# Neighbour lists of a sparse attention layer: 32 strided chunks of 104 columns in place of 52 contiguous chunks of 64

## The chip, the cores and the metric

The kernel runs on one core of a Trainium2 chip. Its time is the device time of one execution, in microseconds (us); the number to judge by is the median of several executions. The profile is one execution recorded by the hardware profiler. Engines are named as there: PE is TensorE, DVE is VectorE, ACT is ScalarE, POOL is GpSimd, SP is SyncE.

## The reference

Four graph attention layers run over n = 3327 nodes with 256 features. The adjacency matrix is given as int32, symmetric, with every node its own neighbour, and sparse: about 33 neighbours per row. Only layer 0 is touched here. It computes

```
g_src = x @ W_src.T + b_src
g_tgt = x @ W_tgt.T + b_tgt
g     = leaky_relu(g_src[:, None, :] + g_tgt[None, :, :], 0.2)
score = einsum('ijc,c->ij', g, a_w)
score = where(adj != 0, score, -inf)
x     = layernorm(x + softmax(score, axis=1) @ g_tgt)
```

The nonlinearity stands between the sum and the product with a_w, so the score of a pair (i, j) can't be split into a part of i and a part of j: each pair costs work over 256 features. Layers 1 to 3 are attention layers whose scores can be split; they are computed densely.

## The kernel before

Layer 0 (`sparse0`) works on the pairs that exist. The nodes are cut into 26 tiles of 128 rows (the last has 127), and the tiles into three sets of 5, 9 and 12 (`SETS`).

`targets` computes g_tgt for each tile and writes it, with one more number per row, to `table_d` in DRAM, 260 numbers per row. The last tile's missing row becomes row n of the table, with a penalty of -1e6: a place in a list that holds no neighbour points there.

`neighbours(s)` makes the lists of one set, one tile after the other. Each half of the adjacency rows (1664 columns) is loaded, and L402 multiplies "is a neighbour" with a descending number, n minus the column, in uint16, so that each neighbour is a distinct positive number and the rest is 0. The same instruction adds the row's numbers up into `sums`. Then the diagonal is taken out (L411, L415). The DVE's MAX8 gives the 8 largest numbers of a row. L421 takes them from each of 52 chunks of 64 adjacent columns. The 3 largest of each chunk (`FIRST`) go to `few` (L426), and the 8 largest of all the fourth to eighth ones too (L430): 52 x 3 + 8 = 164 candidates. L433 and L435 take the 56 largest (`KMAX`) out of `few` in 7 rounds of 8. L440 and L443 subtract what was found from the row's sum; a remainder would set `lost`. At the very end, a branch repeats everything densely (`dense0`) if any row lost a neighbour. L445 turns numbers back into table rows.

Within a set, rows are then sorted by their number of neighbours: PE spreads a key of each row (L466), L475 counts the larger ones, and the lists are written to DRAM in that order (`write_list`, L488) and read back (`read_lists`, L496). Sorting lets each tile of the sorted order gather only as many places as its longest list needs (`LEVELS`), 923 gathers in all.

A gather (L527) is an indirect transfer issued by POOL: for one place of the list it fetches a table row for each of 128 rows. Eight places make a part; 11 buffers hold parts. `score` on DVE takes maxima (L546), multiplies with a_w and sums (L552), and adds a column of the table to the scores (L607). `combine` makes the softmax: DVE finds the largest score (L618), ACT scales the gathered rows (L633) and PE adds them up (L636).

The order on PE, DVE, ACT and POOL is the program's order inside `sparse0`; nothing is moved by a scheduler there. The lists of set 0 are made first, each step of `neighbours(0)` behind one tile of `targets`. Then a loop goes over the parts: in each turn it runs as many steps of the next sets' `neighbours` as are needed to have the lists in time, issues the gather four parts ahead, and scores the current part. `neighbours` gives way 6 times per tile: in the middle and at the end of each half's chunks, after the rounds of `found`, and after the sort key. A set's lists are written by POOL between gathers.

Of the kernel before, what the change touches and what calls it, by code (L numbers as in the profile page):

```python
# [8 lines left out]
F32 = mybir.dt.float32  # L9
# [5 lines left out]
ALU = mybir.AluOpType  # L15
# [4 lines left out]
P = 128  # L20
# [5 lines left out]


KMAX = 56
CHUNK = 64
FIRST = 3  # L30


SETS = (5, 9, 12)
# [13 lines left out]
def gat_stack(  # L47
# [51 lines left out]

    h = [nodes.tile([P, dim], F32, name=f"h{it}") for it in range(nt)]  # L100
    at_d = dram.tile([nt * P, n], BF16, name="at_d")
    table_d = dram.tile([nt * P, ROW], F32, name="table_d")

    def copy_rows(engine, dst, src):

# [141 lines left out]

    def sparse0(lost):  # L250
        GROUP, TURNS, LEAD = 8, 11, 4
        starts = [sum(SETS[:s]) for s in range(len(SETS))]
        with ExitStack() as s0:
# [33 lines left out]
            for lo, hi in halves:  # L287
                hi = -(-hi // P) * P
                rev_i = io0.tile([P, nt * P // 2], I32, tag="adj_i", name="rev_i")
                nc.gpsimd.iota(  # L290
                    rev_i[:, : hi - lo], pattern=[[-1, hi - lo]], base=n - lo,
                    channel_multiplier=0,
                )
                nc.vector.tensor_copy(rev[:, lo:hi], rev_i[:, : hi - lo])
# [37 lines left out]
            def targets(it):  # L332

                xt, pn = columns_of(it)
                row = io0.tile([P, ROW], F32, tag="row", name="row", bufs=3)
                nc.vector.memset(row[:, dim:], 0.0)
                if pn < P:
                    nc.vector.memset(row[:, :dim], 0.0)
                    nc.vector.memset(row[:, dim : dim + 1], -FAR)
                pt = ps0.tile([P, BANK], F32, tag="acc", name="pt")  # L340
                project(pt, xt, pn, w_tgt)
                yield
                nc.vector.tensor_add(row[:pn, :dim], pt[:pn, :dim], bt_row[:pn])
                nc.scalar.copy(row[:pn, dim : dim + 1], pt[:pn, dim : dim + 1])
                nc.scalar.dma_start(table_d[it * P : (it + 1) * P, :], row)
                nc.scalar.dma_start(own_rows(it)[:, 2 * dim :], row)
                yield

# [23 lines left out]
            ]  # L372

            len_c = nt * P // CHUNK

            def neighbours(s):

# [7 lines left out]
                for t in range(size):  # L385
                    it = starts[s] + t
                    pn = rows_of(it)
                    before, of_rows = of_rows, sources(it)
                    cand = io0.tile([P, len_c, 8], F32, tag="cand", name="cand")
                    sums = io0.tile([P, 4], F32, tag="sums", name="sums")  # L390
                    if pn < P:
                        nc.vector.memset(sums, 0.0)
                    for b, (lo, hi) in enumerate(halves):
                        w, padded = hi - lo, -(-(hi - lo) // P) * P
                        adj_i = io0.tile([P, nt * P // 2], I32, tag="adj_i", name="adj_i")
                        copy_rows(nc.sync, adj_i[:pn, :w], adj[it * P : it * P + pn, lo:hi])
                        v = io0.tile([P, wider], U16, tag="num", name="num")
                        if pn < P:
                            nc.vector.memset(v, 0.0)
                        elif w < padded:  # L400
                            nc.vector.memset(v[:, w:padded], 0.0)
                        nc.vector.scalar_tensor_tensor(  # L402
                            v[:pn, :w], adj_i[:pn, :w], 0.0, rev[:pn, lo:hi],
                            op0=ALU.not_equal, op1=ALU.mult, accum_out=sums[:pn, b : b + 1],
                        )
                        if lo <= it * P < hi:

                            at0 = it * P - lo
                            own_v = v[:, at0 : at0 + P]
                            junk = io0.tile([P, P], F32, tag="junk", name="junk")  # L410
                            nc.vector.scalar_tensor_tensor(  # L411
                                junk, own_v, -1.0, ident, op0=ALU.mult, op1=ALU.mult,
                                accum_out=sums[:, 2:3],
                            )
                            nc.vector.tensor_mul(own_v, own_v, off_diag)  # L415
                        chunks = padded // CHUNK
                        for c in range(chunks):
                            if c == chunks // 2:
                                next(of_rows if b else before, None)
                                yield  # L420
                            nc.vector.max(  # L421
                                cand[:, lo // CHUNK + c, :], v[:, c * CHUNK : (c + 1) * CHUNK]
                            )
                        yield
                    few = io0.tile([P, FIRST * len_c + 8], F32, tag="few", name="few")
                    nc.vector.tensor_copy(  # L426
                        few[:, : FIRST * len_c].rearrange("p (c f) -> p c f", f=FIRST),
                        cand[:, :, :FIRST],
                    )
                    nc.vector.max(few[:, FIRST * len_c :], cand[:, :, FIRST:])  # L430
                    found = io0.tile([P, KMAX], F32, tag="found", name="found")
                    for r in range(0, KMAX, 8):
                        nc.vector.max(found[:, r : r + 8], few)  # L433
                        if r + 8 < KMAX:
                            nc.vector.match_replace(  # L435
                                out=few, in_to_replace=found[:, r : r + 8], in_values=few,
                                imm_value=0.0,
                            )
                    yield
                    nc.vector.tensor_reduce(  # L440
                        sums[:, 3:4], found, axis=AX.X, op=ALU.add, negate=True
                    )
                    nc.vector.tensor_reduce(lost[:, it : it + 1], sums, axis=AX.X, op=ALU.add)  # L443
                    payload = io0.tile([P, KMAX + 2], U32, tag=f"pay{t}", name="payload", bufs=1)
                    nc.vector.tensor_scalar(  # L445
                        payload[:, :KMAX], found, -1.0, float(n), op0=ALU.mult, op1=ALU.add
                    )
                    nc.vector.tensor_copy(payload[:, KMAX : KMAX + 1], own_i[:, it : it + 1])
                    nc.vector.tensor_scalar_mul(
                        payload[:, KMAX + 1 :], sums[:, 2:3], -1.0  # L450
                    )
                    payloads.append(payload)

                    junk = io0.tile([P, P], F32, tag="junk", name="junk")
                    count = io0.tile([P, 1], F32, tag="count", name="count")
                    nc.vector.tensor_scalar(
                        junk[:, :KMAX], found, 0.0, 0.0, op0=ALU.is_gt, op1=ALU.add,
                        accum_out=count,
                    )
                    nc.vector.scalar_tensor_tensor(  # L460
                        keys[:, t : t + 1], count, 4096.0, own_f[:, it : it + 1],
                        op0=ALU.mult, op1=ALU.subtract,
                    )
                    key_diag = io0.tile([P, P], F32, tag="key_diag", name="key_diag")
                    nc.vector.tensor_scalar_mul(key_diag, ident, keys[:, t : t + 1])  # L465
                    nc.tensor.matmul(  # L466
                        key_rows[:, t * P : (t + 1) * P], ones, key_diag, start=True, stop=True
                    )
                    yield
# [93 lines left out]
            def score(q):  # L563
# [6 lines left out]
                if k0 == 0:  # L570
                    sc = entry["sc"] = io0.tile([P, KMAX + 1], F32, tag="sc", name="sc", bufs=3)
                    if kt < KMAX:
                        at = nt + starts[s] + t
                        nc.vector.tensor_scalar(
                            lost[:, at : at + 1], entry["lst"][:, kt : kt + 1], float(n), None,
                            op0=ALU.is_lt,
                        )

                    y_own = io0.tile([P, 1, dim], F32, tag="y_own", name="y_own", bufs=1)
# [129 lines left out]
            def finish(s):  # L709
                mv, rstd = moments.pop(s)  # L710
                for k in range(SETS[s]):
                    it = starts[s] + k
                    pn = rows_of(it)
                    nc.vector.tensor_scalar(
                        h[it][:pn], h[it][:pn], mv[:pn, k, 0:1], rstd[:pn, k : k + 1],
                        op0=ALU.subtract, op1=ALU.mult,
                    )


            first = neighbours(0)  # L720
# [782 lines left out]
```

The softmax here doesn't subtract the row's maximum and nothing guards it: scores larger than these inputs give would overflow.

## Time and profile before

| what | value |
|---|---|
| median of 3 executions | 3261.68 us (3260.0 to 3262.12) |
| span of the profiled execution | 3261.5 us |
| PE busy | 2224.4 us, 68% of the span |
| DVE busy | 2318.1 us, 71% |
| POOL busy | 1029.6 us, 32% |
| first and last gather (L527) | 166.9 us and 1515.0 us |
| MAX8 over chunks (L421) | 1352, mean 209 ns |
| MAX8 and MATCH_REPLACE8 over `few` (L433, L435) | 182 and 156, mean 332 and 313 ns |

The shares over the span mix stages: up to about 1515 us the kernel is in layer 0, after it in the dense layers, where PE is nearly always busy. A stage has to be read by itself. The durations of DVE's instructions overlap, one starting before the one before it has ended, so a group's count times its mean is more than its busy time. A row of the view of waits reads: engine, what it was about to do, the work it waited for, the time in all, how often, the longest.

### The profile page before, as it was taken

The numbers are of one execution on the slowest core, as the hardware profiler recorded it, in microseconds if no ns is written. First come the engines' busy times: TensorE is split into PE (matmuls) and PEld (weight loads), VectorE is DVE, ScalarE is ACT, GpSimd is POOL, SyncE is SP. The second block draws the span as 40 slices with busy tenths as digits, with TensorE's granted clock in tenths as the row PEclk, the third lists the DMA queues.
The fourth block names the chain that finished last, engine by engine and source line by source line (L and its number), as shares of the span: only waits on it lengthen the run. The fifth ranks groups of instructions, "written<-read, shape, count | busy, mean of one in ns | idle before, by whom it ended". The sixth has DMA issues, their size and how long they took to land.

```text
span 3261.5 us, 44647 instructions
## 1 busy us (share of the span) xinstructions
PE 2224.4 (68%) x15644; PEld 1218.1 (37%) x15644; DVE 2318.1 (71%) x6589; ACT 741.5 (23%) x2002; POOL 1029.6 (32%) x1034
## 2 busy tenths in 40 slices
PE   3203332343441444343899999999999999999997
PEld 2101111121220221111478888774334444334342
DVE  6789999999975655554235642117888788899998
ACT  0003231342341343333334431110111110110110
POOL 0077657777767777774000000000000000000000
PEclk7556666666765776676699999999999999999998
DMA  7466536555435444443466753332212212212111
GB/s 216 137 141 180 169 100 150 173 157 155 112 86 109 124 111 113 113 113 91 125 199 199 201 161 93 100 99 72 63 44 68 61 46 65 63 49 57 56 47 48
DMA packets 176842, 364.21 MB, mean 112 GB/s; under 512 B 33746, under 2 KB 118964, under 8 KB 176610
## 3 DMA queue, kind: packets, MB, share of 16 engines
q1 hardware_dynamic: 96682, 183.56, 19.8%
q0 software_dynamic: 49632, 141.57, 16.9%
q10 hardware_dynamic: 30296, 36.15, 3.2%
q8 instruction: 126, 2.06, 0.3%
q14 instruction: 106, 0.87, 0.1%
HBM read 320.99 MB, written 43.58 MB: 112 GB/s over the span
## 4 chain that ended last, share of the span: by engine, by line
PE 46%; DVE 4%; DMA 2%; ACT 1%; issue 1%; DVEq 0%; SPq 0%; POOL 0%; ACTq 0%; POOLq 0%
PE acc L1198 17%; PE acc L1159 15%; PE acc L1206 8%; PE misc L1011 3%; DVE e L1075 3%; PE misc L1048 1%; DMA at_i<-in_adj_t_dram 1%; PE misc L1104 1%; DMA at<-at_d 1%; PE misc L1280 0%; PE misc L1241 0%; PE acc L636 0%; DVE stats L1355 0%; DVE h L1353 0%; ACT feat L1023 0%
## 5 line engine op out<-in xcount | busy, mean ns | idle before, releaser
L527 POOL DMA_INDIRECT g<-table_d,lst x923 | 912.6, 989 | 295.6 <-issue 268.8
L1075 DVE SCALAR_TENSOR_TENSOR e<-rate,feat,at 128x896 f32<-128x896 f32 (+4 forms) x832 | 843.1, 1078 | 67.7 <-PE acc L1206 58.4
L636 PE MATMUL acc<-g,ident 128*128 128x512 f32 (+1 forms) x934 | 454.7, 644 | 545.2 <-ACT g L633 512.7
L1198 PE MATMUL acc<-e,feat 128*32 128x384 f32 (+2 forms) x6656 | 722.8, 514 | 5.2 <-DVE e L1075 2.4
L225 POOL TENSOR_TENSOR rstds<-rstds,minus_half 128x7 f32<-128x7 f32 (+1 forms) x12 | 19.6, 1633 | 1671.7 <-DVE rstds L224 1671.7
L636 PEld LDWEIGHTS acc<-g,ident 128*128 128x128 f32 x934 | 193.3, 211 | 783.7 <-ACT g L633 561.6
L546 DVE TENSOR_TENSOR y<-g,both 128x1024 f32<-128x1024 f32 (+2 forms) x240 | 276.0, 1173 | 238.4 <-DMA g<-table_d,lst 223.5
L1206 PE MATMUL acc<-e,feat 128*32 128x384 f32 (+3 forms) x3328 | 397.5, 512 | 0.0
L1198 PEld LDWEIGHTS acc<-e,feat 128*32 128x32 f32 x6656 | 245.1, 109 | 381.8 <-issue 262.5
L633 ACT ACTIVATE g<-g,w 128x256 f32<-128x256 f32 x923 | 370.6, 494 | 0.0
L552 DVE SCALAR_TENSOR_TENSOR y<-y,both 128x256 f32<-128x256 f32 x923 | 324.5, 415 | 0.0
L1159 PE MATMUL acc<-feat,e 128*128 128x257 f32 (+2 forms) x1352 | 307.4, 381 | 0.6 <-DVE h L1173 0.6
L1159 PEld LDWEIGHTS acc<-feat,e 128*128 128x128 f32 (+2 forms) x1352 | 253.2, 190 | 39.7 <-issue 4.1
L1159 PE MATMUL acc<-feat,at 128*128 128x257 bf16 (+2 forms) x2028 | 240.9, 276 | 7.5 <-DMA at<-at_d 7.3
L466 PE MATMUL key_rows<-key_diag,ones 128*128 128x128 f32 x52 | 17.8, 440 | 314.5 <-DVE key_diag L465 259.5
L1159 PEld LDWEIGHTS <-at 128*128 128x128 bf16 (+2 forms) x2028 | 200.2, 100 | 43.9 <-DMA at<-at_d 8.0
L1075 DVE SCALAR_TENSOR_TENSOR e<-rate,feat,at_i 128x896 f32<-128x896 f32 (+2 forms) x104 | 112.2, 1081 | 143.1 <-DMA at_i<-in_adj_t_dram 109.8
L1206 PEld LDWEIGHTS acc<-e,feat 128*32 128x32 f32 (+1 forms) x3328 | 136.1, 110 | 164.2 <-issue 150.4
L421 DVE MAX8 cand<-num 128x8 f32<-128x64 uint16 x1352 | 178.9, 209 | 1.0
L542 ACT COPY both<-own_of 128x256 f32<-128x256 f32 x26 | 9.7, 374 | 602.1 <-DMA own_of<-own_d,lst 469.2
L466 PEld LDWEIGHTS key_rows<-key_diag,ones 128*128 128x128 f32 x52 | 12.1, 278 | 327.8 <-DVE key_diag L465 216.0
L1092 ACT CAST at<-at_i 128x896 bf16<-128x896 int32 (+2 forms) x104 | 92.0, 885 | 108.5 <-DMA at_i<-in_adj_t_dram 104.2
(158 smaller groups left out, 1707.5 us busy)
## 6 DMA issues: line engine op xcount, KB each, us to landing
at<-at_d SPq DMA_DIRECT2D x150, 224.0 KB
at_i<-in_adj_t_dram SPq DMA_DIRECT2D x50, 448.0 KB
adj_i<-in_adj_dram SPq DMA_DIRECT2D x25, 832.0 KB
adj_i<-in_adj_dram SPq DMA_DIRECT2D x25, 831.5 KB
g<-table_d,lst POOLq DMA_INDIRECT x923, 2.8
at<-at_d SPq DMA_DIRECT2D x75, 192.0 KB
at<-at_d SPq DMA_DIRECT2D x75, 191.8 KB
at_d<-at ACTq DMA_DIRECT2D x50, 224.0 KB
```

The source lines that it names most:

```text
L421: nc.vector.max(cand[:, lo // CHUNK + c, :], v[:, c * CHUNK : (c + 1) * CHUNK])
L527: nc.gpsimd.indirect_dma_start(out=g[:, k - k0, :], out_offset=None, in_=table_d[:, :], in_offset=bass.IndirectOffsetOnAxis(ap=entry["lst" ...
L546: nc.vector.tensor_tensor(y, rows, minus_src[:, None, :].to_broadcast([P, m, dim]), op=ALU.max)
L552: nc.vector.scalar_tensor_tensor(y, y, 1.0, a, op0=ALU.mult, op1=ALU.mult, accum_out=sc)
L633: nc.scalar.activation(rows, rows, AF.Copy, scale=w[:, k : k + 1])
L636: nc.tensor.matmul(dst, ident, rows, start=start, stop=stop)
L1011: nc.tensor.matmul(pacc[:pn, : dim + nh], ht[:, k, :pn], self.weight[:, k, :], start=(k == 0), stop=(k == kc - 1),)
L1075: nc.vector.scalar_tensor_tensor(e[:pn, : c1 - c0], self.rate[b][:pn, h_of, : c1 - c0], q, at[:pn, : c1 - c0], op0=ALU.max, op1=ALU.mult,)
L1092: nc.scalar.copy(at[:pn, :w], at_i[:pn, :w])
L1159: nc.tensor.matmul(accs[s][:pn, : dim + 1], a[:pj, s * P : s * P + pn], f[:pj, : dim + 1], start=(j == 0 and part == 0), stop=(j == nt - 1 ...
L1198: nc.tensor.matmul(accs[x][p][q : q + 32, : hi - lo], f[:pj, at0 : at0 + 32], es[at0 // hd][:pj, lo:hi], start=(j == 0), stop=(j == nt - 1),)
L1206: nc.tensor.matmul(accs[x][pairs][h_of * 32 : (h_of + 1) * 32, : hi - lo], f[:pj, dim + h_of : dim + h_of + 1].to_broadcast([pj, 32]), es[ ...
```

## The change

A chunk becomes 104 columns, so there are 32 and not 52. A chunk's columns are no longer adjacent: in a half with 16 chunks, chunk c holds columns c, c + 16, c + 32 and so on. Adjacent chunks of this length would have more rows with many neighbours in one chunk. `few` then has 32 x 3 + 8 = 104 candidates, and one more: the row's sum less the sum of the candidates. If just one neighbour is not among the candidates, this difference is that neighbour's number. A bound keeps it in range where several are missing, which the check on `lost` still finds.

For the numbers to be told from sums more easily they are now 4096 plus the column, ascending, so a list runs from high columns to low ones. The absent neighbour becomes row 0 of the table, all real rows move down by one, and the row with the penalty is written once at the start. The list arithmetic follows.

```diff
-CHUNK = 64
+CHUNK = 104
 FIRST = 3
+BASE = 4096
...
-    table_d = dram.tile([nt * P, ROW], F32, name="table_d")
+    assert n <= BASE
+    table_d = dram.tile([n + 1, ROW], F32, name="table_d")
...
-                    rev_i[:, : hi - lo], pattern=[[-1, hi - lo]], base=n - lo,
+                    rev_i[:, : hi - lo], pattern=[[1, hi - lo]], base=BASE + lo,
...
-                    nc.vector.memset(row[:, dim : dim + 1], -FAR)
...
-                nc.scalar.dma_start(table_d[it * P : (it + 1) * P, :], row)
+                nc.scalar.dma_start(table_d[1 + it * P : 1 + it * P + pn, :], row[:pn])
...
                         chunks = padded // CHUNK
+                        spread_v = v[:, :padded].rearrange("p (i c) -> p c i", c=chunks)
...
                             nc.vector.max(
-                                cand[:, lo // CHUNK + c, :], v[:, c * CHUNK : (c + 1) * CHUNK]
+                                cand[:, lo // CHUNK + c, :], spread_v[:, c, :]
                             )
                         yield
-                    few = io0.tile([P, FIRST * len_c + 8], F32, tag="few", name="few")
+                    few = io0.tile([P, FIRST * len_c + 9], F32, tag="few", name="few")
...
-                    nc.vector.max(few[:, FIRST * len_c :], cand[:, :, FIRST:])
+                    nc.vector.max(few[:, FIRST * len_c : FIRST * len_c + 8], cand[:, :, FIRST:])
+
+                    nc.vector.tensor_reduce(
+                        sums[:, 3:4], few[:, : FIRST * len_c + 8], axis=AX.X, op=ALU.add, negate=True
+                    )
+                    lack = few[:, FIRST * len_c + 8 :]
+                    nc.vector.tensor_reduce(lack, sums, axis=AX.X, op=ALU.add)
+                    nc.vector.tensor_scalar_min(lack, lack, float(BASE + n - 1))
...
-                        payload[:, :KMAX], found, -1.0, float(n), op0=ALU.mult, op1=ALU.add
+                        payload[:, :KMAX], found, 1.0 - BASE, 0.0, op0=ALU.add, op1=ALU.max
...
-                            lost[:, at : at + 1], entry["lst"][:, kt : kt + 1], float(n), None,
-                            op0=ALU.is_lt,
+                            lost[:, at : at + 1], entry["lst"][:, kt : kt + 1], 0.0, None,
+                            op0=ALU.is_gt,
...
+            none = io0.tile([1, ROW], F32, tag="pen", name="none")
+            nc.vector.memset(none, 0.0)
+            nc.vector.memset(none[:, dim : dim + 1], -FAR)
+            nc.scalar.dma_start(table_d[0:1, :], none)
```

More of the change, by code (lines that the diff above doesn't have):

```diff
@@ L374, in sparse0 @@
             len_c = nt * P // CHUNK
+            assert all((-(-hi // P) * P - lo) % CHUNK == 0 for lo, hi in halves)
             def neighbours(s):
```

## The prediction

> **What bounds the kernel now.** I read the page's 40 slices first (VectorE, the DVE, fills its slices up to about 900 us and TensorE only from 1600 us on), then cut the span into stages and asked for each engine's busy time in each:
>
> ```profile
> 26.00:142.00 116.00, 45.91 (x122) 31.25 (x122) 101.56 (x519) 3.98 (x25) 0.19 (x1) 0.63 0.58 172
> 142.00:190.00 48.00, 0.00 (x1) 0.04 (x1) 22.87 (x113) 0.75 (x2) 26.15 (x26) 0.50 0.35 98
> 190.00:905.00 715.00, 253.94 (x568) 122.54 (x568) 694.34 (x3044) 186.81 (x478) 507.65 (x492) 0.65 0.54 148
> 905.00:1515.00 610.00, 244.22 (x512) 109.88 (x512) 348.65 (x1309) 212.39 (x544) 462.24 (x485) 0.69 0.43 112
> 1515.00:3261.00 1746.00, 1674.41 (x14426) 949.90 (x14426) 1145.96 (x1592) 336.16 (x951) 25.80 (x17) 0.97 0.32 91
> ```
>
> The columns are stage, length, then PE, PEld, DVE, ACT and POOL busy. From 26 to 142 us DVE works 101.56 of 116 us, on the lists of the first 5 tiles. From 190 to 905 us it works 694.34 of 715 us (97%): the lists of the other 21 tiles, mixed with scores. From 905 us on DVE has air, and GpSimd's queue (POOL) issues one gather each 1.25 us to the end of layer 0. Everything after 1515 us is layers 1 to 3, which the change doesn't touch. So the question is what POOL waits for before 905 us. The view of its waits says:
>
> ```profile
> POOL lists_d L488 <- DVE ranks_i L479: 133.7, 1, 133.7
> POOL lists_d L488 <- DVE lost L574: 24.8, 1, 24.8
> POOL lists_d L488 <- DVE inv L658: 11.5, 1, 11.5
> ```
>
> Each of the three sets ends with one wait of POOL for DVE's ranks, before it may write the lists (L488). In the timeline the second ends at 431.98 us, just after ranks_i at 431.53, though the row names a neighbour instruction; the third ends at 905.71. A longer DVE lengthens all three one for one. A shorter one can take back no more than the wait that is there: 11.5 us in the last set.
>
> **What one DVE instruction costs.** Duration isn't what counts, as instructions overlap; the distance between starts is. From the timeline and the groups by form:
>
> ```profile
> 28.41 1.74 DVE L421 MAX8 cand<-num 128x8 f32<-128x64 uint16 x13
> 38.49 0.43 DVE L430 MAX8 few<-cand 128x8 f32<-128x260 f32 x1
> 38.95 0.33 DVE L433 MAX8 found<-few 128x8 f32<-128x164 f32 x1
> 44.29 0.20 DVE L440 TENSOR_REDUCE sums<-found 128x1 f32<-128x56 f32 x1
> 44.53 0.16 DVE L443 TENSOR_REDUCE lost<-sums 128x1 f32<-128x4 f32 x1
> ```
> ```profile
> L421 DVE MAX8 cand<-num 128x8 f32<-128x64 uint16 x1352 | 178.9, 209 | 1.0
> ...
> L607 DVE TENSOR_TENSOR sc<-sc,g 128x2 f32<-128x2 f32 x3 | 0.5, 161 | 0.1
> L607 DVE TENSOR_TENSOR sc<-sc,g 128x4 f32<-128x4 f32 x2 | 0.3, 166 | 0.1
> L607 DVE TENSOR_TENSOR sc<-sc,g 128x7 f32<-128x7 f32 x1 | 0.2, 171 | 0.0
> L618 DVE TENSOR_REDUCE top<-sc 128x1 f32<-128x57 f32 x3 | 0.6, 211 | 0.1
> L618 DVE TENSOR_REDUCE top<-sc 128x1 f32<-128x27 f32 x1 | 0.2, 181 | 0.0
> ```
>
> Thirteen MAX8 of 64 elements take 1.74 us with the last one's 0.209, so one follows the other after (1.74 - 0.21)/12 = 127 ns. An adjacent element costs 1.04 ns on this engine: L546 takes 411 ns for 256 and 1214 for 1024, and L618 gives (211 - 181)/30 = 1.0. So 127 ns is 67 for 64 elements and 60 fixed.
>
> L607 is the row that decides this case. It adds column dim of the gathered rows, elements that lie 1040 bytes apart. From 2 to 7 of them it grows by 10 ns, 2.0 each; a line through its rows of 2 to 7 (161, 163, 166, 169, 168, 171) gives 1.94. That is about two cycles of 1.04 for each element that lies alone. The new chunks read v with a step of 16 uint16, 32 bytes, so here too no two elements are neighbours.
>
> [...]
>
> **The change, part by part, for one tile of 128 rows.**
> - Chunk search (L421): before 52 x 127 = 6.60 us. After, 32 of 104 elements. At two cycles: 60 + 104 x 2.08 = 276 ns, 32 x 276 = 8.84 us, +2.24. At one cycle: 60 + 108 = 168 ns, 5.38 us, -1.22. I take two cycles, for a measured row of this engine stands behind it.
> - Search in few: 164 candidates become 105, 59 x 1.04 = 61 ns off each of 7 MAX8 (L433) and 6 MATCH_REPLACE8 (L435), both contiguous at one element per cycle: -0.80. L430 reads 160, not 260: -0.10. The copy L426 moves 96, not 156, about -0.03.
> - Three new instructions, each waiting for the one before, and the first MAX8 of few queued behind them. The sum over 104: L440 to L443 is 0.24 us for 56, plus 48 x 1.04 = 0.05: 0.29. The sum over 4: 0.157 as L443 and the same 0.035 of hand-over: 0.19. The minimum, like L449 (0.15) with a hand-over: 0.19. Together +0.67.
> - All but the chunks: 0.67 - 0.93 = -0.26 us. With two cycles +1.98 us per tile, with one -1.48.
> - The list arithmetic (L445, L574) keeps its instructions and shapes, so costs nothing. The absent row is written once at the start: two memsets and one small transfer, while DVE waits 15.5 us for the first adjacency. The last table transfer now has 127 rows; the last issue is at 122.6 us and the first gather at 166.9, so even a transfer several times slower stays hidden behind the ranks and the lists.
> - The gathers stay 923. Lists now run downward, which changes the rows' order and not their number.
> - The fallback branch runs only if a list lacks an entry. Counted on the seeded matrix, no row has over 8 neighbours in a strided chunk, and none over 7 beyond three per chunk, where 8 places wait. It stays off.
>
> **The sum.** 26 tiles x 1.98 = +51 us. It lies wholly on the path: 5 tiles (+9.9) before the first gather, 9 (+17.8) before the second ranks, 12 (+23.8) before the third. Nothing hides it, as DVE has no air there. 3261.7 + 51.5 = 3313 us.
>
> **Rivals.**
> - One cycle per strided element. For it: [...]L607's few elements, whose small growth might be start-up. Against it: the contiguous L618 grows by half as much on shapes nearly as small. Then 5 x 1.48 = 7.4 at the start, 9 x 1.48 = 13.3 of the 24.8 us wait, and in the last set 17.8, of which the wait holds only 11.5, since POOL becomes the bound there: -32 us, 3229 us. This is the other side: faster.
> - The gathers set the pace already, and longer searches hide behind them. For it: POOL between its stops issues at its full pace, 1.25 us per gather. Against it: the stops of 24.8 and 11.5 us end on DVE, so they would only grow. Then the start alone pays: 3261.7 + 9.9 = 3272 us.
> - A step of 32 bytes costs more than 1040 did, say four cycles[...]. 60 + 104 x 4.17 = 493 ns, 15.8 us per tile, +8.9 with the rest, 26 x 8.9 = +232, 3494 us.
>
> **How the numbers follow.** Two cycles or nearly so 0.80, one cycle 0.14, gathers as the bound 0.03, four cycles 0.03. The size of a strided element is the one unknown that makes the range: 1.7 ns gives 60 + 177 = 237 ns, 7.57 us, +0.71 per tile, +18 us (3280); 2.45 ns gives 315 ns, 10.1 us, +3.2, +83 us (3345). The coarse start distance of L607 with 8 elements, 0.08 us less some 60 fixed, allows such a value above 2.08. The range 3280 to 3345 leaves out the rivals at 0.14, 0.03 and 0.03, hence 0.20. Faster 0.14 is the one-cycle case; within 0.2% is 0.03, a strided element of about 1.5 ns; slower is the rest, 0.83.
>
> **What would show it.** In the changed profile MAX8 of the chunks should number 832 and follow each other after about 276 ns: eight in a row in about 2.3 us with the last one's length. 168 ns says one cycle, 490 four. The searches in few should stand about 61 ns lower each, and the sum over 104 at about 0.26 us long. POOL's wait for the first ranks should grow by 10 us to about 144, the second to about 43, the third to about 35, and the time from the third wait's end to the last gather stay at 610 us. The prediction is wrong if the strided read costs what a plain one does, or if the waits of POOL don't grow with DVE's work.

## The result and the profile after

The changed kernel takes 3289.88 us (median of 4 executions, 3285.5 to 3293.01), the kernel before, beside it on the same chip, 3261.9 us. The ratio is 1.0085, with a 95% interval of 1.0068 to 1.0102: slower by about 28 us, where +51 was forecast.

The same stages in the changed kernel, each cut where the same piece of work begins or ends; the columns are as before:

```profile
26.00:147.50 121.50, 47.26 (x122) 32.43 (x122) 106.40 (x433) 3.98 (x25) 0.17 (x1) 0.61 0.57 164
147.50:195.50 48.00, 0.00 (x0) 0.00 (x0) 23.69 (x96) 0.75 (x2) 26.57 (x26) 0.50 0.34 97
195.50:933.30 737.80, 252.82 (x568) 122.08 (x568) 715.33 (x2705) 186.74 (x478) 505.07 (x492) 0.65 0.53 144
933.30:1543.10 609.80, 245.42 (x512) 110.16 (x512) 348.74 (x1309) 212.40 (x544) 462.02 (x486) 0.69 0.44 112
1543.10:3285.00 1741.90, 1668.30 (x14426) 947.89 (x14426) 1146.23 (x1592) 336.25 (x951) 25.78 (x17) 0.98 0.32 91
```

The first stage has become 5.5 us longer. The stage in which DVE mixes lists and scores has become 23 us longer, at 97% busy as before, although DVE issues 339 instructions fewer in it. The gather stage behind it is as long as it was. The time was lost where the lists are made, and POOL's queue shows when. These are its first list of each set and its last gather, in the timeline of the kernel before and then of the changed kernel (there with the write of one tile's sums, L684, which matters further down):

```profile
141.81 2.44 POOL L488 DMA_INDIRECT lists_d<-payload,ranks_i  x1 [133.70 <-DVE ranks_i L479]
431.98 0.99 POOL L488 DMA_INDIRECT lists_d<-payload,ranks_i  x1 [24.84 <-DVE lost L574]
905.71 1.00 POOL L488 DMA_INDIRECT lists_d<-payload,ranks_i  x1 [11.48 <-DVE inv L658]
1515.02 0.95 POOL L527 DMA_INDIRECT g<-table_d,lst  x1 [0.30 <-issue]
```
```profile
147.33 2.44 POOL L501 DMA_INDIRECT lists_d<-payload,ranks_i  x1 [139.02 <-DVE ranks_i L492]
418.59 0.99 POOL L684 DMA_INDIRECT sums_d<-hs,lst  x1 [5.78 <-DVE hs L677]
447.03 0.99 POOL L501 DMA_INDIRECT lists_d<-payload,ranks_i  x1 [24.92 <-DVE lost L587]
934.04 1.00 POOL L501 DMA_INDIRECT lists_d<-payload,ranks_i  x1 [15.90 <-DVE inv L671]
1543.09 0.94 POOL L540 DMA_INDIRECT g<-table_d,lst  x1 [0.30 <-issue]
```

The first list of set 0 goes out 5.5 us later than before, that of set 1 15.1 us later, that of set 2 28.3, the last gather 28.1. From the third list to the last gather it is 609 us in both. So each tile's list costs about 1.1 us more, and nothing gives it back.

The groups by form and one tile of the timeline show what DVE does differently:

```profile
L427 DVE MAX8 cand<-num 128x8 f32<-128x104 uint16 x832 | 212.9, 330 | 1.8
L446 DVE MAX8 found<-few 128x8 f32<-128x105 f32 x182 | 49.2, 271 | 6.3
```
```profile
28.19 2.06 DVE L427 MAX8 cand<-num 128x8 f32<-128x104 uint16 x8
39.55 0.32 DVE L436 MAX8 few<-cand 128x8 f32<-128x160 f32 x1
39.90 0.26 DVE L438 TENSOR_REDUCE sums<-few 128x1 f32<-128x104 f32 x1
40.20 0.16 DVE L442 TENSOR_REDUCE few<-sums 128x1 f32<-128x4 f32 x1
40.38 0.15 DVE L443 TENSOR_SCALAR few<-few 128x1 f32<-128x1 f32 x1
40.57 0.27 DVE L446 MAX8 found<-few 128x8 f32<-128x105 f32 x1
```

Eight chunk searches take 2.06 us: (2.06 - 0.33) / 7 = 247 ns from start to start; the median over the trace is 245, and of the kernel before 126. Per tile that is 32 x 245 = 7.84 us in place of 52 x 126 = 6.55: +1.29. The search in `few` became 61 ns shorter per instruction (271 for 332), 13 times, and L436 0.10. The copy into `few` and the search behind it stand 0.12 us apart and not 0.15 (0.03). The new chain stands from 39.90 to 40.57, 0.67 us. Together 1.29 - 0.79 - 0.10 - 0.03 + 0.67 = +1.04 us, and 26 tiles make 27 us.

### The profile page after: what moved, and what is told of

Its sections match the earlier page's. It is cut to its first block, busy times and chain, and to the rows that moved or that the text cites. A ratio compares the mean times of both kernels' runs of the same rounds, so it can differ in the third digit from the quotient of the medians.

```text
span 3285.9 us, 44206 instructions
## 1 busy us (share of the span) xinstructions
PE 2219.9 (68%) x15644; PEld 1216.8 (37%) x15644; DVE 2345.6 (71%) x6148; ACT 741.6 (23%) x2002; POOL 1027.3 (31%) x1034
## 3 DMA queue, kind: packets, MB, share of 16 engines
q8 instruction: 126, 2.06, 0.3%
## 4 chain that ended last, share of the span: by engine, by line
PE 45%; DVE 4%; DMA 2%; ACT 1%; issue 1%; DVEq 0%; ACTq 0%; POOL 0%; POOLq 0%; SPq 0%
PE acc L1216 17%; PE acc L1177 15%; PE acc L1224 8%; PE misc L1029 3%; DVE e L1093 3%; PE misc L1066 1%; DMA at_i<-in_adj_t_dram 1%; PE misc L1122 1%; DMA at<-at_d 1%; PE misc L1298 0%; PE misc L1259 0%; PE acc L649 0%; DVE stats L1373 0%; DVE h L1371 0%; ACT feat L1041 0%
## 5 line engine op out<-in xcount | busy, mean ns | idle before, releaser
L646 ACT ACTIVATE g<-g,w 128x256 f32<-128x256 f32 x923 | 370.6, 494 | 0.0
L427 DVE MAX8 cand<-num 128x8 f32<-128x104 uint16 x832 | 212.9, 330 | 1.8
```

Source lines behind the costliest of these rows:

```text
L427: nc.vector.max(cand[:, lo // CHUNK + c, :], spread_v[:, c, :])
L646: nc.scalar.activation(rows, rows, AF.Copy, scale=w[:, k : k + 1])
```

## The experiments

They ran on other chips than the result (e1 to e4 on one, e5 to e8 on a second, e9 and e10 on a third, e11 and e12 on a fourth), and there is one thing to know first. On those chips the kernel before took about 3660 to 3695 us. In its profile there (e11) the changed kernel took 426 us more than on the first chip: 280 us of that lie between POOL's first list and its first list of the third set, 119 between there and the last gather. DVE's next instruction was late at times, without a wait that the profile knows ("issue"), or behind one whose end it can't name ("remote"). These are lines of e11, from the view of DVE's waits and from the timeline:

```profile
DVE y L565 <- issue: 170.1, 172, 2.4
```
```profile
262.93 2.06 DVE L427 MAX8 cand<-num 128x8 f32<-128x104 uint16 x8 [9.33 <-remote]
266.40 0.35 DVE L427 MAX8 cand<-num 128x8 f32<-128x104 uint16 x1 [1.41 <-issue]
267.80 0.35 DVE L427 MAX8 cand<-num 128x8 f32<-128x104 uint16 x1 [1.05 <-issue]
269.20 0.35 DVE L427 MAX8 cand<-num 128x8 f32<-128x104 uint16 x1 [1.05 <-issue]
269.90 0.34 DVE L427 MAX8 cand<-num 128x8 f32<-128x104 uint16 x1 [0.36 <-issue]
```

The eight searches of the first line run 247 ns apart, and the next ones follow each other after 1.4, 1.4 and 0.7 us. So whole times from these chips are set against the kernel before on the same chip, by ratio, and they hold some time that is not DVE's work. Before the first gather no such lateness shows. From the first look at adjacency (L402, in the changed kernel L406) to the first list on POOL, the changed kernel takes 147.33 - 25.60 = 121.73 us on the first chip and 147.98 - 26.25 = 121.73 on another. That stretch holds five tiles of list work and nothing of gathers, and it is the measure used here; the kernel before takes 141.81 - 25.82 = 115.99.

| kernel | MAX8, start to start | to the first list | per tile against before | ratio to before, 95% |
|---|---|---|---|---|
| before | 126 ns | 115.99 us | | |
| changed (first chip) | 245 | 121.73 | +1.15 us | 1.0085 (1.0068 to 1.0102) |
| e11, changed again | 245 | 121.73 | +1.15 | 1.0085 (1.0056 to 1.0115) |
| e1, adjacent columns | 168 | 108.80 | -1.44 | 0.9916 (0.9884 to 0.9948) |
| e2, step of 4 | 168 | 109.20 | -1.36 | 0.9926 (0.9897 to 0.9955) |
| e3, step of 8 | 242 | 121.16 | +1.03 | 1.0029 (1.0013 to 1.0046) |
| e4, pairs | 168 | 109.29 | -1.34 | 0.9942 (0.9922 to 0.9961) |
| e5, pairs again | 168 | 109.31 | -1.34 | 0.9954 (0.9937 to 0.9971) |
| e6, no extra candidate | 245 | 118.18 | +0.44 | 0.9997 (0.9982 to 1.0013) |
| e7, the rest of the change | 126 | 116.01 | 0.00 | 1.0008 (0.9980 to 1.0036) |
| e8, pairs, no extra candidate | 168 | 105.80 | -2.04 | 0.9924 (0.9896 to 0.9952) |
| e10, the same again | 168 | 105.83 | -2.03 | 0.9921 (0.9905 to 0.9938) |
| e9, before with a step of 26 | 169 | 127.54 | +2.31 | 1.0177 (1.0144 to 1.0210) |
| e12, lists first | 245 | 121.69 | +1.14 | 1.0074 (1.0054 to 1.0094) |

Start to start is the median distance of neighbouring starts in the trace; per tile is the difference of the third column from 115.99, divided by 5.

**Is it the step?** e1 makes a chunk of adjacent columns again, 104 of them.

```diff
-spread_v = v[:, :padded].rearrange("p (i c) -> p c i", c=chunks)
+spread_v = v[:, :padded].rearrange("p (c i) -> p c i", c=chunks)
...
-nc.vector.tensor_scalar_min(most[:, 0:1], most[:, 0:1], 1.0)
+nc.vector.tensor_scalar_min(most[:, 0:1], most[:, 0:1], 0.0)
```

> The changed kernel, but a chunk is 104 adjacent columns again; one row then lacks three neighbours in its list, and the dense repetition is switched off, so that row's result is not the reference's. Theory 1 (the stepped read is what costs): the chunk MAX8 follow each other after 60 + 104 x 1.04 = 168 ns and not 245, 32 x 77 ns = 2.46 us less per tile, 64 us of DVE in all. In the last set POOL's stops of 26 us hold no more than that of the 29.6, so about 60 us less than the changed kernel, 3229 us. Theory 2 (MAX8 of 104 uint16 is slow whatever the step): 245 ns stays and the time stays at 3290.

```profile
28.00 1.45 DVE L427 MAX8 cand<-num 128x8 f32<-128x104 uint16 x8
```

Same count, same length, and 1.45 us for eight where the change took 2.06. The distance is 168 ns, as 60 + 104 x 1.04 says. Theory 2 falls. The stretch to the first list is 12.9 us shorter than the change's, 2.6 per tile, and shorter than before's too. The whole time is 31 us less than the kernel before takes on this chip, where the expectation had put 33.

**Which steps cost?** e2, e3 and e4 keep 104 columns per chunk and change how they lie (the new lines alone are shown).

```diff
 # e2: s = 4, e3: s = 8
+spread_v = v[:, :padded].rearrange("p (b i c) -> p b c i", c=s, i=CHUNK)
+    cand[:, lo // CHUNK + c, :], spread_v[:, c // s, c % s, :]
 # e4
+spread_v = v[:, :padded].rearrange("p (i c t) -> p c i t", c=chunks, t=2)
+    cand[:, lo // CHUNK + c, :], spread_v[:, c, :, :]
```

> The changed kernel with a step of 4 elements (8 bytes) in blocks of 416 columns, everything else the same. Theory 1a [...]168 ns as without a step, about 3229 us. Theory 1b (any step other than one costs): 245 ns, 3290 us.

> The changed kernel with a step of 8 elements (16 bytes[...]) in blocks of 832 columns. Theory 1a: as the change, 245 ns and 3290 us. Theory 1c (it is the 32-byte step[...] that costs): near 168 ns, 3229 us.

> The changed kernel, a chunk being pairs of adjacent columns with a step of 16 pairs (64 bytes) between them: 52 pairs[...]. Theory 1a: [...]about 168 ns and 3229 us. Theory 1b [...]60 + 147 = 207 ns, 32 x 38 ns = 1.2 us less per tile, 32 us in all, 3258 us.

The first eight searches of e2, of e3 and of e4:

```profile
28.16 1.45 DVE L427 MAX8 cand<-num 128x8 f32<-128x104 uint16 x8
```
```profile
28.14 2.03 DVE L427 MAX8 cand<-num 128x8 f32<-128x104 uint16 x8
```
```profile
27.55 1.44 DVE L427 MAX8 cand<-num 128x8 f32<-128x104 uint16 x8
```

A step of 8 bytes costs nothing (168 ns in e2, as adjacent columns in e1); a step of 16 bytes costs nearly what 32 does (242 ns in e3, 245 in the change); pairs with 64 bytes from one to the next cost nothing (168 in e4). Theory 1a, which expects 168, 245 and 168 ns of the three, holds within 3 ns. e2 rules out 1b, e3 rules out 1c, and e4 rules out the 207 ns, in which one element of each pair was put at 1.78 ns and the other at 1.04. With the fixed 60 kept, an element took (168 - 60) / 104 = 1.04 ns in e1, e2 and e4, 1.75 in e3 and 1.78 in the change. No run has a step between 8 and 16 bytes, and none shows what makes the difference.

The whole times have the expected signs but not the sizes. e2 and e4 were expected 1.0% below the kernel before and came out 0.7 and 0.6% below it; e3 was expected 0.9% above it, like the changed kernel, and came out 0.3% above. Where the rest went on these chips is not shown.

**Per element or per instruction?** e9 takes the kernel before and only spreads its chunks.

```diff
-cand[:, lo // CHUNK + c, :], v[:, c * CHUNK : (c + 1) * CHUNK]
+cand[:, lo // CHUNK + c, :], v[:, :padded].rearrange("p (i c) -> p c i", c=chunks)[:, c, :]
```

> The kernel before with one thing changed: each of its 52 chunks of 64 takes every 26th column (52 bytes) and not adjacent ones. My theory, with the size measured on the changed kernel (60 fixed + 1.78 per element that lies alone): 60 + 64 x 1.78 = 174 ns and not 126 from start to start, 52 x 48 ns = 2.5 us more per tile, 65 us of DVE in 26 tiles, 3327 us where the kernel before takes 3262. The rival that the price is one more fixed amount per instruction (245 - 168 = 77 ns) and not one per element: 203 ns, 4.0 us per tile, 104 us, 3366.

```profile
27.92 2.29 DVE L421 MAX8 cand<-num 128x8 f32<-128x64 uint16 x13
```

The distance is 169 ns: 43 more than adjacent for 64 elements, where 104 cost 77 more. A fixed amount is excluded. Between 64 and 104 elements the spread ones grow by (245 - 169) / 40 = 1.9 ns each, the adjacent ones by (168 - 126) / 40 = 1.05; the line through the former starts at 47 ns and not at 60. That line has two points only, at different steps (52 and 32 bytes), and e3 shows that the step alone can move the distance by 3 ns. With the fixed 60 kept, the two points give 1.70 and 1.78 ns per element. Which of the two forms holds is not settled. The whole time rose by 1.8% there, 63.5 us, close to the 65 expected.

**What do the other parts cost?** e6 leaves out the three new instructions; e7 also goes back to 52 adjacent chunks of 64, so that only the numbers, the list order and the table's new row and transfers stay changed. The diff shows the instructions left out; `few` becomes one place shorter with them.

```diff
 # e6 and e7
-nc.vector.tensor_reduce(sums[:, 3:4], few[:, : FIRST * len_c + 8], ..., negate=True)
-nc.vector.tensor_reduce(lack, sums, axis=AX.X, op=ALU.add)
-nc.vector.tensor_scalar_min(lack, lack, float(BASE + n - 1))
 # e7 besides
-CHUNK = 104
+CHUNK = 64
-spread_v = v[:, :padded].rearrange("p (i c) -> p c i", c=chunks)
+spread_v = v[:, :padded].rearrange("p (c i) -> p c i", c=chunks)
```

> The changed kernel without the extra candidate: the sum over 104, the sum over 4 and the minimum are left out, and no row needs that candidate on this matrix. By the starts, 0.296 + 0.192 + 0.188 = 0.68 us less per tile, 17.6 us in all: 3272 us. If the three instructions lie in time in which DVE would wait anyway, 3290.

> What is left of the change with 52 chunks of 64 adjacent columns, and without the extra candidate: ascending numbers from 4096, the table's row 0 for an absent neighbour, the last transfer of 127 rows, lists that run downward. My theory: it costs nothing, 3262 us within 5. The rival: another order of the gathers or the absent row at the table's head costs or saves something; then the time after the third ranks differs from 610 us.

To the first list, e6 is 3.55 us shorter than the change, 0.71 per tile, where the starts gave 0.68. In the whole time it can't be told from the kernel before on its chip, while 10 us more was expected. This can't be read as a miss of the price, since the same chip has lateness of the size in question (e6 175 us in one row of DVE's waits). e7 needs 116.01 us where the kernel before needs 115.99, and the interval of its ratio holds 1 (0.9980 to 1.0036). From the third list to the last gather it takes 715 us, within the 713 to 734 us of the other variants on these chips. So the rest costs nothing that can be measured.

**A version that beats both.** e5 repeats e4 in the hope of a chip without the lateness; e8 and e10 join pairs with the three instructions left out.

> The changed kernel with its chunks made of pairs of adjacent columns, as in the run before, for its time where DVE's instructions do not come late. The chunk MAX8 stand 168 ns apart, so DVE has 32 x 77 ns = 2.46 us less per tile than the changed kernel and 1.44 us less than the kernel before: 64 and 37 us in 26 tiles. If DVE sets the pace up to the last ranks, 3226 to 3232 us; if POOL's gathers do, little of it is seen and the time stays near 3262.

> Pairs of adjacent columns and no extra candidate: against the kernel before 1.44 + 0.68 = 2.12 us less of DVE per tile, 55 us in all, 10.6 of it before the first list, 19 in the second set and 25 in the third. POOL's stops in the third set are only 16.5 us in the kernel before, so if they are the limit about 46 us come through, 3216 us; if DVE's work alone counts, 3207.

> Pairs of adjacent columns and no extra candidate, once more, in the hope of a chip on which DVE's instructions do not come late: there 3207 to 3216 us against 3262 of the kernel before. Where they do come late, a ratio near 0.992 as in the run before, since part of DVE's time is then not its work.

No chip without lateness was met. e5 repeats e4's stretch to 0.02 us and again is faster than before, by 0.5% where 0.9 to 1.1% was expected without lateness. e8 and e10 save 2.04 us per tile (2.12 expected) and are 0.8% faster than the kernel before, twice: with 104 columns in pairs the fewer, longer searches do pay. Of the 46 to 55 us of DVE's work expected, 28 arrive. The expectation had a cap for the third set: POOL would stop waiting for DVE and its own pace would hold. In both profiles POOL still waits for DVE there, in e8 and in e10:

```profile
POOL lists_d L495 <- DVE inv L665: 24.6, 1, 24.6
POOL lists_d L495 <- DVE inv L665: 25.6, 1, 25.6
```

So at that list the cap was not reached. That the lateness took the rest fits this, but no run separates it, and what these two kernels give on the first chip wasn't seen.

**Why POOL's waits for ranks grew so little.** I had forecast that they would take up DVE's whole delay. In the changed kernel the second was 24.92 us, as before (24.84). The timeline above shows a reason: POOL's write of one tile's sums (L684) stands before the first list in its queue, and waits for a row that DVE writes some 28 us before the ranks. POOL can't arrive earlier. e12 puts the lists of the second and of the third set ahead of the sums that are queued with them (and writes the lists of a set in reverse order); e11 is the changed kernel beside it.

```diff
-at_step(at, between.append, lambda s=s, it=it: write_list(s, it))
+at_step(at, between.insert, 0, lambda s=s, it=it: write_list(s, it))
```

> The changed kernel itself, so that the variants have it beside them where DVE's instructions come late. If such a chip only adds waiting and leaves DVE's work on the path, some 27 us above the kernel before as on the first chip, ratio 1.007 to 1.008. If lateness depends on the number of instructions, the changed kernel, which has 441 fewer on DVE, loses less: nearer to the 1.003 of the variant with a step of 8.

> The changed kernel, in which POOL writes the second set's lists ahead of one tile's sums, so that nothing which DVE writes shortly before the ranks stands before the first list in POOL's queue. My theory: POOL's wait for the second ranks is held at 24.9 us only because POOL waits for those sums just before; now the wait for the ranks takes over that one as well, and is over 30 us, while DVE and the time stay as they were. The rival: the wait for the ranks is as long as DVE's sort takes, and stays at 25.

The waits of POOL in e11, and then in e12:

```profile
POOL sums_d L684 <- DVE hs L677: 106.9, 7, 28.3
...
POOL lists_d L501 <- DVE lost L587: 24.9, 1, 24.9
POOL lists_d L501 <- DVE inv L671: 24.6, 1, 24.6
```
```profile
POOL sums_d L684 <- DVE hs L677: 88.3, 7, 27.5
POOL lists_d L501 <- DVE lost L587: 39.7, 1, 39.7
POOL lists_d L501 <- DVE inv L671: 24.7, 1, 24.7
```

The wait for the second ranks takes over what stood before the sums and is 39.7 us, while e12's ratio (1.0074) can't be told from that of e11. So the row's length says where POOL stands in its queue, and not how much DVE is late. For the third set the edit moved nothing: the wait is 24.7 us and 24.6 in e11, and what holds it there stays open. e11 gives the same ratio as the first chip, 1.0085. Of its two expectations the first holds for e11: the change's loss isn't made up by its fewer instructions. It is no rule for such chips, since e3 and e6 lost less there than their list work.

## Why the prediction was right, and where it was off

- *What bounds the kernel.* Right. DVE's work up to the ranks came through in full: +5.5, +15.1 and +28.3 us at the three lists by 5, 14 and 26 tiles, and the gather stage kept its 609 us. In the rival in which the gathers set the pace, the delay would have stopped growing after the first 5.5.
- *A spread element costs more than an adjacent one.* Right at the change's step of 32 bytes (245 ns against e1's 168) and at 16 (242, e3); at 8 bytes and in pairs it does not (168, e2 and e4). The prediction calls a cycle the 1.04 ns that an adjacent element adds (L546, L618). The rival of one cycle per element, whose 0.14 was my estimate, would have given 168 ns to the changed kernel; e1, e2 and e4 have that, and save 6.7 to 7.2 us in the first five tiles against the kernel before, where the rival had put 7.4.
- *Its size.* Off: the term "32 x 276 = 8.84 us, +2.24" was mis-sized. It measured 32 x 245 = 7.84 us, +1.29 (the 127 of before is 126). In the changed kernel an element adds (245 - 60) / 104 = 1.78 ns and not 2.08. L607's rows had said 1.94; I rounded them to 2.08, twice an adjacent element. The rounding is 104 x 0.14 = 15 of the 31 ns that the distance was off. The other 16 lie in the slope carried over from L607 or in the full 60 added to it; e9 does not separate the two. The rival of 4.17 ns per element falls: it put the distance at 493 ns.
- *The row that decided.* Its choice was in part luck. The line through L607's rows left out the ones and the eights, and the eights are 106 of its 126 instructions:

```profile
L607 DVE TENSOR_TENSOR sc<-sc,g 128x8 f32<-128x8 f32 x106 | 17.7, 167 | 0.2
```

  Taken as it stands, this row makes the growth from 2 to 8 elements 1.0 ns each, no more than an adjacent element costs. The prediction gave no reason for leaving it out. There is one in the trace: 100 of the eights stand behind other instructions than the shorter ones do. The six that follow L552, as all the shorter ones do, have a median of 171.5 ns, the three ones a median of 159: (171.5 - 159) / 7 = 1.8 ns per element. So like set beside like would have given nearly the measured 1.78.
- *The three new instructions, and what became shorter.* Right: +0.67 forecast; 0.67 in the timeline, 0.71 by e6. -0.80 forecast for the search in `few`, -0.79 measured.
- *What was costed at nothing.* Right, by e7.
- *The sum.* 26 x 1.98 became 26 x 1.04 = 27 us by the starts, 28 by the median. The one mis-sized term explains all of the distance, 26 x (2.24 - 1.29) = 25 us. The range had been made from that term's bounds, and holds because its lower one stood at 1.7 ns per element.
- *POOL's waits.* Wrong in their form: 144, 43 and 35 us were forecast, 139.0, 24.9 and 15.9 came. The first is right for the smaller size. For the second the step "A longer DVE lengthens all three one for one" failed, and with it one of the signs that were to show the prediction wrong: this wait did not grow with DVE's work, although the list was 15.1 us late. The delay lies in earlier waits of POOL. Between the first lists of the first and the second set, its gathers' wait for ACT's scaling (L646) was 6.7 us and before 3.3, that for the sums 5.8 and before 4.8, and the longest one put down to "issue" 7.9 and before 2.5; e12 shows that the sums hold the wait for the ranks at 25 us. In the third set the wait for the ranks grew by 4.4 us, and the gathers' waits for ACT from 0.6 to 11.5. The same error sits in the rival that capped the gain of a faster DVE at 11.5 us in the last set, since it counted one stop of POOL alone; how much could be taken back there on the first chip was not measured.

## What to carry to other kernels

Before spreading a reduction over strided columns, look at how far each element lies from the next one taken: in MAX8 over 104 uint16 on VectorE a step of 8 bytes cost nothing (168 ns), steps of 16 and 32 bytes cost 0.7 ns more per element (242 and 245), and a layout in pairs 64 bytes apart kept the spread for nothing (168). The price was in the profile beforehand, in a small row that nobody would look at for its time: the growth of a strided instruction over its sizes, set against that of an adjacent one. Such a row has to be read with like beside like: the same instruction before it, and every size that there is. And take the moment at which a queue gets past a wait, not the length of the wait, as the measure of how late the other engine is.

## What the runs showed of the hardware

- MAX8 over 104 uint16: 168 ns from start to start with a step of 1 or 4 elements or in pairs, 242 with a step of 8, 245 with 16. Over 64: 126 adjacent, 169 with a step of 26.
- On all the other chips the kernel before took 12 to 13% longer. In e11, on one of them, the searches from 266.40 to 275.50 us started 1.4 or 0.7 us apart; the median over that trace is 245 ns. What holds them up stays open; no run here separates it.
